# Eight-sequence transformer block on one core: gate denominators, moments, stacks, divisions and projections placed elsewhere in the order of the work, and the first sequence's attention visits put between whole units

## The chip, the cores and the metric

The kernel runs on one core of a Trainium2 chip. Time is device time in microseconds for one execution of the whole program. Three runs of the kernel before took 641.94, 647.98 and 648.69 us; their median, 647.98 us, is the figure to compare with.

## The reference: what is computed

Input is x with 8 sequences of 512 positions and 256 features, float32. Both branches work on the layer norm of x:

```python
xn = _layernorm(x, axis=-1)
s = _L0_attn_ref(xn, in_proj_w, out_proj_w)
g = _silu(_L0_ffn_ref(xn, k0, k1, k2, s0, s1, s2))
return x + s * g

# attention: 16 heads of 16, rotary embedding on q and k
delta = pos[:, None] - pos[None, :]
mask = (delta >= 0) & (delta < 250)
attn = softmax(where(mask, q @ k.T * 16 ** -0.5, min))
s = (attn @ v) @ out_proj_w.T

# feed-forward: weights are +1 or -1, chosen by booleans
h = concatenate([xn, -xn])            # 512
h = relu(s0 * h @ w0) * 2             # 1024
h = relu(s1 * h @ w1) * 2             # 1024
g = s2 * h @ w2                       # 256, then silu
```

The attention is a sliding window: a position sees itself and the 249 before it.

## The kernel before, in words

**Layout.** Everything runs with features on the partitions and the 512 positions along the row. A sequence has 2 chunks of 128 features in and out, and 8 chunks of 128 hidden features.

**Feed-forward.** A hidden layer is computed in units: unit f of `h1` makes hidden chunk f from the normed input, unit f of `h2` makes it from all eight chunks of `h1`. To keep float32 accuracy each operand is split into an f16 high part (`xh`, `h1h`, `h2h`) and a low part of a reduced float32 (`xl`, `h1l`, `h2l`), and each product is done for both. So an `h2` unit is two halves of 8 matmuls of 128x512, high and low (L511). Its result is read by ScalarE (ACT), which writes the high part (L522), and then by VectorE (DVE), which writes the low part (L520) and so releases the bank of the accumulator. The last layer (L562, `z_ps`) makes `gate` u = 0 and 1, one for each output chunk.

**Gate.** silu(g) is g / (1 + exp(-g)). `gate_ready` (L623) does it: load of the residual `xr` (L545, a DMA on the SP queue), exp on ACT into `den` (L627), +1 on GpSimd (POOL, L631), the reciprocal in two halves on DVE (L636), and the product on POOL (L638). There is one `den` buffer, and both gates of a sequence use it.

**Attention.** q and k of a sequence are projected (`ka_ps`, `kb_ps`, `qa_ps`, `qb_ps`, L381), multiplied by the rotary tables on DVE (L397), added up on POOL (L418), split into high and low parts (ACT L434, DVE L441), and written to DRAM (L427). `stack` (L450) loads them back in the arrangement that the scores need, one pair of k and q tiles for each group of heads, four groups. The scores are then done in six visits a sequence (`step`): 12 matmuls into six `sc` banks (L745), six exps on ACT (L770), masks on POOL (L790, L797), and in the next visit the products with v into `po` (L827). `keep` copies `po` out (odd groups on DVE L845 and L846, even ones on ACT L851 and L852). `divisions` then sends the row sums through DRAM to pack them (gather L915, pack L923), inverts them on DVE (L929), unpacks them (L942) and multiplies `V` by them (shuffle on DVE L948, product on POOL L949). `project_o` makes `att_ps` (L959), multiplies it with the gate (DVE L981), adds the residual (POOL L988) and stores (L989).

**Norm of the next sequence.** For all but the first, `load_xT` loads the transposed input, `stats` and `lay_down` compute mean and deviation and write these moments to DRAM (L289), `lay_over` broadcasts them to all partitions as `of_all` (L298, 512 KB), and `norm_turned` does, for each of two chunks c, (x - mean) * rstd on DVE (L309, two operations), `xh` on ACT (L315) and `xl` on DVE (L313).

**The order of the work.** Nothing is scheduled by the compiler. `everything` is a list of pieces (nominal time, cost, function). `run` sorts them by nominal time and calls them in that order; its clock advances by the costs, and what a piece returns is called with a delay after it. The resulting order is kept on each engine: PE, DVE, ACT, POOL and the SP queue each take their instructions strictly as emitted. A sequence has `SEQ` = 42 units of nominal time; an `h1` unit costs `L1` = 0.87, an `h2` unit `L2` = 3.45 (emitted as two halves of 1.725, first the f16 matmuls, then the reduced ones), and a `z` product `L3` = 1.87. In the time of sequence b the engines do the attention and the `h2` units of b, the last layer, the gates and the output of b-1, and norm and projections of b+1. The nominal times of those are in `prepare` (norm, k, q, v), `finish_ffn` and `late` (gates, `att_ps`) and `divisions`.

**Places of the visits.** `attention` puts the six visits evenly among the pieces of its sequence by cost: for b > 0 only in front of a piece whose time is in `quick` (the start of a whole unit), for b = 0 in front of any piece. It puts the four `stack` calls at times derived from the visits; tiles for stacks have two buffers, so a group can be loaded when the last visit of the group two before it has been reached.

**Accumulator banks.** Seven banks of one tag serve `h_ps`, `sc` (six in a visit), `z_ps`, `att_ps` and all projections in turn; an eighth holds `po`. A product on PE can begin when the seventh bank before has been read out, whoever reads it.

Of the kernel before, what the change touches and what calls it, by code (L numbers as in the profile page):

```python
# [34 lines left out]
def tile_attention_times_gated_ffn(  # L35
# [44 lines left out]
    B, T, E = x.shape  # L80
# [140 lines left out]
    SEQ = 42.0  # L221
# [1 line left out]
    states = {}  # L223


    quick = set()

    def warm(count_):

# [223 lines left out]
    def prepare(b, plain=False):  # L453

        if b == 0 or plain:
            at = dict(stats=-40, norm=-38, x=-36, k=0, q=3, v=9.2)
            dp, dv = 1.5, 1.5
        else:

            at = dict(load=9, stats=9, down=10.5, over=12, norm=16.8, k=21.8, q=24.8, v=SEQ + 0.6)  # L460
            if b == 1:
                at.update(load=18.65, stats=15, down=18, over=18.7, norm=24.8, k=26.6, q=28.4)
            dp, dv = 1.5, 0.85
            at = {n: SEQ * (b - 1) + f for n, f in at.items()}
        out = [(at["stats"], 0, lambda: stats(b))]
        if "over" in at:
            out += [
                (at["load"], 0, lambda: load_xT(b)), (at["down"], 0, lambda: lay_down(b)),
                (at["over"], 0, lambda: lay_over(b)),
                (at["norm"], 0, lambda: norm_turned(b, 0)),  # L470
                (at["norm"] + 1.2, 0, lambda: norm_turned(b, 1)),
            ]
        for t in range(NT):
            if "over" not in at:
                out += [
                    (at["norm"] + t, 0, lambda t=t: norm(b, t)),
                    (at["x"] + t, 0.25, lambda t=t: turn_x(b, t, plain)),
                ]
            out.append((at["v"] + dv * t, 0.87, lambda t=t: project_v(b, t)))
        for what in "kq":  # L480
            for n, part in enumerate("ab"):
                if b == 0 and what == "k" and not plain:

                    out += [
                        (-34.3 if n == 0 else -32.95, 0.87, lambda p=part: project(b, "k", p, 0)),
                        (at["k"] + dp * n, 0.87, lambda p=part: project(b, "k", p, 1)),
                    ]
                else:
                    out.append((
                        at[what] + dp * n, 1.75, lambda w=what, p=part: project(b, w, p),  # L490
                    ))
        return out
# [54 lines left out]
    def last(b, u, how):  # L547
        st = states[b]
        f, cols = outputs(b)[u]
        pz = bank(f"z_ps_{b}_{u}")  # L550
        if b + 1 == B:
            pz = pz[:, : T // 2]
        if how == "at once":
            for c in range(NF1):
                nc.tensor.matmul(
                    pz, w2[:, c, ts(f, P)].bitcast(F32), st["h2p"][:, c, cols],
                    start=(c == 0), stop=(c == NF1 - 1),
                )
        else:
            for p in "hl":  # L560
                for c in range(NF1):
                    nc.tensor.matmul(  # L562
                        pz, weights(w2, p, c, ts(f, P)), st["h2" + p][:, c, cols],
                        start=(c == 0 and p == "h"), stop=(c == NF1 - 1 and p == "l"),
                    )
        if cols.start == 0:
            st["gate of", f] = outs.tile([P, T], F32, tag=f"gate{f}", name=f"gate_{b}_{f}")
        gate = st["gate", u] = st["gate of", f][:, cols]
        if how == "final":
            residual(b, u)  # L570
            den = beside(b, u, "den")

            halves = [ts(k, T // 4) for k in range(2)]

            def ends():
                if u == 2:
                    for k in halves:
                        nc.scalar.activation(
                            den[:, k], pz[:, k], AF.Exp, scale=scales[:, 1:2]
                        )  # L580
                    return [(0.1, ready)]
                nc.scalar.activation(den, pz, AF.Exp, scale=scales[:, 1:2])
                nc.scalar.activation(den, den, AF.Identity, bias=1.0)
                return [(0.88, ready)]

            def ready():
                if u == 2:
                    for k in halves:
                        nc.vector.tensor_scalar(den[:, k], den[:, k], 1.0, None, ALU.add)
                        nc.vector.reciprocal(den[:, k], den[:, k])  # L590
                else:
                    nc.vector.reciprocal(den, den)  # L592
                nc.vector.scalar_tensor_tensor(  # L593
                    gate, pz, scales[:, 0:1], den, ALU.mult, ALU.mult
                )

            return [(0.0, ends)]

        def scale():
            nc.vector.tensor_scalar(gate, pz, scales[:, 0:1], None, ALU.mult)  # L600
            if how != "later":
                return [(7.5 if u == 0 else 11.0, lambda: gate_ready(b, u))]

        return [(0.0, scale)]

# [16 lines left out]

    def gate_ready(b, u):  # L623
        st = states[b]
        residual(b, u)
        gate, den = st["gate", u], beside(b, u, "den")
        nc.scalar.activation(den, gate, AF.Exp, scale=-1.0)  # L627
        width = T // 2 if b + 1 == B else T

        def add():  # L630
            nc.gpsimd.tensor_scalar(den, den, 1.0, None, ALU.add)  # L631
            return [(0.9 + 1.1 * k, lambda k=k: invert_(k)) for k in range(2)]

        def invert_(k):
            part = den[:, ts(k, width // 2)]
            nc.vector.reciprocal(part, part)  # L636
            if k == 1:
                return [(1.8, lambda: nc.gpsimd.tensor_tensor(gate, gate, den, ALU.mult))]  # L638

        return [(0.5, add)]  # L640
# [11 lines left out]
    def late(b, u):  # L652

        if b + 1 == B:
            return last_at(b, 3) + L3 + 0.9 * u
        return SEQ * (b + 1) + (33.5 + 6.4 * u if b + 2 < B else 19.2 + 5.0 * u)

    def finish_ffn(b, u, how):
        quick.add(last_at(b, u))
        out = [(last_at(b, u), L3 * (2 if b + 1 < B else 1), lambda: last(b, u, how))]  # L660
        if how == "later":
            out.append((late(b, u) - 4.5, 0, lambda: gate_ready(b, u)))
        return out

    def ffn(b):

        now = SEQ * b + (NT * L3 if b == 0 else 0)
        out = []
        for f in range(NF0):
            quick.add(now)  # L670
            out.append((now, L1, lambda f=f: layer(b, "h1", "x", w0, f)))
            now += L1
            if f % 4 == 3 and b > 0:
                now += 2 * L3
        if b + 1 == B:
            for half in range(2):
                cols = ts(half, T // 2)
                for f in range(NF1):
                    quick.add(now)
                    out.append((  # L680
                        now, L2 / 2,
                        lambda f=f, cols=cols: layer(b, "h2", "h1", w1, f, cols=cols),
                    ))
                    now += L2 / 2
                now += 2 * L3
            return out
        for f in range(NF1):
            quick.add(now)
            for i in range(2):
                out.append(  # L690
                    (now, L2 / 2, lambda f=f, i=i: layer(b, "h2", "h1", w1, f, i, 2))
                )
                now += L2 / 2
        return out
# [172 lines left out]

    def attention(b, among):

        first, end = SEQ * b + (20.6 if b == 0 else 0.0), ends_at(b)  # L870
        inside = sorted((at, cost) for at, cost, _ in among if first <= at < end)
        whole = sum(cost for _, cost in inside)
        times, done = [], 0.0
        places = {}
        for at, cost in inside:
            if at in quick or b == 0:
                places[at] = done
            done += cost
        for n in range(len(steps)):
# [6 lines left out]
        for g in range(NG):  # L886

            at = times[used[g - 2][-1]] + 0.01 if g > 1 else first - (
                3.5 if b == 0 else 4.0 if b == 1 else 9.0
            )  # L890
            if b and g == 1:
                at = first + 0.01
            out.append((at, 0, lambda g=g: stack(b, g)))
# [108 lines left out]
    def divisions(b, pairs=(0, 1)):  # L1002
        out = []
        for pair in pairs:
            if b + 1 < B:
                first = SEQ * b + 30.0 if pair == 0 else SEQ * (b + 1) + 3.0
            else:
                first = SEQ * b + (22.5 if pair == 0 else 33.4)
            pieces = (gather, pack, invert, unpack, divide)
            very_last = b + 1 == B and pair == 1  # L1010
            for f, at in zip(
                pieces, (0.0, 2.0, 4.4, 6.4, 9.0) if very_last else (0.0, 2.4, 5.2, 7.6, 10.6)
            ):
                out.append((first + at, 0, lambda p=pair, f=f: f(b, p)))
        return out
# [183 lines left out]
```

## Time and profile before

| | us |
|---|---|
| median of 3 runs | 647.98 |
| profiled execution | 648.76 |
| span of the profiled execution | 647.0 |
| busy PE (matmul) | 606.3 (94%) |
| busy DVE | 331.4 (51%) |
| busy ACT | 293.1 (45%) |
| busy POOL | 289.8 (45%) |
| mean granted PE clock | 0.976 |

The span is the time from the first to the last instruction in the trace; the rest of the 648.76 us lies around it. The page cuts the span into 40 slices; the digits are the busy share in tenths, and PEclk is the granted clock in tenths:

```profile
PE   7979979999898998989999898999989989899996
DVE  7834324544544554454634556345653655435346
ACT  3745544535345444544436345353444435365511
POOL 2746431456424454245432455344462435625623
PEclk9989989999899998999989999999999999899999
```

PE is nearly full everywhere, with a slice below full about every fifth; the other three are half full, unevenly. After the first sequence the pattern has a period of about 78.5 us, that of one sequence, until the last.

### The profile page before, as it was taken

The numbers are of one execution on the slowest core, as the hardware profiler recorded it, in microseconds if no ns is written. First come the engines' busy times: TensorE is split into PE (matmuls) and PEld (weight loads), VectorE is DVE, ScalarE is ACT, GpSimd is POOL, SyncE is SP. The second block draws the span as 40 slices with busy tenths as digits, with TensorE's granted clock in tenths as the row PEclk, the third lists the DMA queues.
The fourth block names the chain that finished last, engine by engine and source line by source line (L and its number), as shares of the span: only waits on it lengthen the run. The fifth ranks groups of instructions, "written<-read, shape, count | busy, mean of one in ns | idle before, by whom it ended". The sixth has DMA issues, their size and how long they took to land. (4 is left out here: it accounts for less than half of the span.)

```text
span 647.0 us, 10374 instructions
## 1 busy us (share of the span) xinstructions
PE 606.3 (94%) x3788; PEld 374.5 (58%) x3788; DVE 331.4 (51%) x578; ACT 293.1 (45%) x555; POOL 289.8 (45%) x490
## 2 busy tenths in 40 slices
PE   7979979999898998989999898999989989899996
PEld 6644546555565555555555554654546645566785
DVE  7834324544544554454634556345653655435346
ACT  3745544535345444544436345353444435365511
POOL 2746431456424454245432455344462435625623
PEclk9989989999899998999989999999999999899999
DMA  8774443337333463325434263350734408322101
GB/s 267 285 241 147 187 153 113 99 129 249 116 100 99 164 214 117 100 99 226 153 117 125 73 261 117 121 165 31 278 117 147 151 14 305 124 87 83 52 17 59
DMA packets 50086, 92.24 MB, mean 143 GB/s; under 512 B 10992, under 2 KB 18672, under 8 KB 50032
## 3 DMA queue, kind: packets, MB, share of 16 engines
q1 hardware_dynamic: 47600, 89.31, 40.8%
q10 hardware_dynamic: 2432, 2.23, 1.1%
q8 instruction: 31, 0.51, 0.3%
q14 instruction: 23, 0.19, 0.1%
HBM read 53.22 MB, written 38.30 MB: 141 GB/s over the span
## 5 line engine op out<-in xcount | busy, mean ns | idle before, releaser
L770 ACT ACTIVATE p<-sc 128x512 f32<-128x512 f32 (+2 forms) x288 | 149.2, 604 | 62.5 <-PE sc L745 61.9
L790 POOL TENSOR_SCALAR_AFFINE_SELECT p<-p 128x256 f32<-128x256 f32 (+1 forms) x224 | 100.3, 458 | 149.3 <-ACT p L770 144.7
L511 PE MATMUL h_ps<-h1l,w_sb 128*128 128x512 f32 (+1 forms) x576 | 146.7, 396 | 0.0
L511 PE MATMUL h_ps<-h1h,w_sb 128*128 128x512 f16 (+1 forms) x576 | 124.6, 360 | 11.0 <-ACT p L770 9.0
L511 PEld LDWEIGHTS h_ps<-h1l,w_sb 128*128 128x128 f32 x576 | 100.4, 189 | 30.6 <-issue 10.4
L511 PEld LDWEIGHTS <-w_sb 128*128 128x128 f16 x704 | 62.0, 98 | 95.9 <-issue 51.8
L522 ACT ACTIVATE h2h<-h_ps 128x512 f16<-128x512 f32 (+1 forms) x72 | 39.6, 550 | 142.7 <-PE h_ps L511 142.7
L827 PE MATMUL po<-p,v_pad 128*32 128x378 f32 (+4 forms) x1152 | 83.0, 429 | 0.0
L745 PE MATMUL sc<-q,k 64*128 64x378 f32 (+4 forms) x576 | 59.6, 319 | 20.4 <-DVE gate L981 10.3
L636 DVE RECIPROCAL den<-den 128x256 f32<-128x256 f32 (+1 forms) x32 | 52.6, 1645 | 45.8 <-POOL den L631 45.8
L745 PEld LDWEIGHTS sc<-q,k 64*128 64x128 f32 x576 | 45.9, 187 | 44.1 <-issue 23.0
L520 DVE SCALAR_TENSOR_TENSOR h1l<-h_ps,h1h 128x512 fp32r<-128x512 f32 x64 | 43.2, 688 | 48.3 <-ACT h1h L522 48.2
L520 DVE SCALAR_TENSOR_TENSOR h2l<-h_ps,h2h 128x512 fp32r<-128x512 f32 (+1 forms) x72 | 43.9, 611 | 44.5 <-ACT h2h L522 44.5
L522 ACT ACTIVATE h1h<-h_ps 128x512 f16<-128x512 f32 x64 | 37.6, 602 | 53.5 <-PE h_ps L511 53.5
L797 POOL TENSOR_SCALAR_AFFINE_SELECT p<-p 128x256 f32<-128x256 f32 x144 | 59.9, 416 | 0.4 <-POOL p L790 0.4
L511 PE MATMUL h_ps<-xl,w_sb 128*128 128x512 f32 x128 | 52.3, 489 | 0.0
L827 PEld LDWEIGHTS po<-p,v_pad 128*32 128x32 f32 x1152 | 35.4, 124 | 27.8 <-issue 20.4
L638 POOL TENSOR_TENSOR gate<-gate,den 128x512 f32<-128x512 f32 (+1 forms) x16 | 19.3, 1206 | 56.4 <-issue 29.0
L949 POOL TENSOR_TENSOR V<-V,R 128x512 f32<-128x512 f32 x16 | 20.3, 1271 | 48.9 <-DVE R L948 48.9
L511 PE MATMUL h_ps<-xh,w_sb 128*128 128x512 f16 x128 | 38.5, 383 | 0.0
L562 PE MATMUL z_ps<-h2l,w_sb 128*128 128x512 f32 (+1 forms) x144 | 35.7, 389 | 0.0
L418 POOL TENSOR_TENSOR m_ka<-m_ka,m_kb 128x512 f32<-128x512 f32 x16 | 19.9, 1266 | 35.1 <-DVE m_kb L397 35.1
(102 smaller groups left out, 668.8 us busy)
## 6 DMA issues: line engine op xcount, KB each, us to landing
k<-dk SPq DMA_DIRECT2D x64, 256.0 KB
q<-dq SPq DMA_DIRECT2D x64, 256.0 KB
dk<-kh SPq DMA_DIRECT2D x16, 512.0 KB
dk<-m_ka SPq DMA_DIRECT2D x16, 512.0 KB
dq<-qh SPq DMA_DIRECT2D x16, 512.0 KB
dq<-m_qa SPq DMA_DIRECT2D x16, 512.0 KB
x<-in_x_dram SPq DMA_DIRECT2D x30, 128.0 KB
xT<-in_x_t_dram SPq DMA_DIRECT2D x7, 512.0 KB
```

Source lines behind the costliest of these rows:

```text
L418: nc.gpsimd.tensor_tensor(m[:, i], m[:, i], n[:, i], op)
L511: nc.tensor.matmul(ph, weights(w, p, c, ts(f, P)), st[src + p][:, c, cols], start=(k == 0), stop=(k == n - 1),)
L520: nc.vector.scalar_tensor_tensor(lo, ph, 0.0, hi, ALU.max, ALU.subtract)
L522: high = lambda: nc.scalar.activation(hi, ph, AF.Relu)
L562: nc.tensor.matmul(pz, weights(w2, p, c, ts(f, P)), st["h2" + p][:, c, cols], start=(c == 0 and p == "h"), stop=(c == NF1 - 1 and p == "l"),)
L636: nc.vector.reciprocal(part, part)
L745: nc.tensor.matmul(sc[r + (4 if y else 2 * pair)][:, ds(at, n)], st["k", g, pair][row, ts(j, P)], st["q", g, pair][row, ds(j * P + first, n)],
L770: nc.scalar.activation(p, s_, AF.Exp, scale=D ** -0.5)
L790: nc.gpsimd.affine_select(out=block, in_=block, compare_op=ALU.is_ge, fill=0.0, base=0, pattern=[[0, heads], [1, P]], channel_multiplier=-1,)
L797: nc.gpsimd.affine_select(out=block, in_=block, compare_op=ALU.is_ge, fill=0.0, base=-1, pattern=[[0, heads], [-1, beyond]], channel_multi ...
L827: nc.tensor.matmul(po[32 * r : 32 * r + 32, ds(j * P + first, n)], v_columns(j, g, r), place(tiles_, r, y, off, n), start=(j == 0), stop=( ...
L949: return [(0.5, lambda: nc.gpsimd.tensor_tensor(V, V, R, ALU.mult))]
```

## The change

The change alters no operation, tile or buffer. It alters nominal times and so the order of instructions on the engines:

- the residual's load is a piece of its own instead of the start of `gate_ready`;
- `gate_ready` of the middle sequences moves from 4.5 to 6.6 ahead of `late`, of the last but one to 4.6, and `late` of gate 1 from 6.4 to 4.9 units after that of gate 0;
- `norm` of sequences 2 to 7 goes from 16.8 to 18.4, k from 21.8 to 23.0 and q from 24.8 to 26.0; of sequence 1, k from 26.6 to 28.1 and q from 28.4 to 31.6, with the two parts of a projection at nearly one time (dp 0.01);
- the visits of the first sequence begin at 24.7 instead of 20.6 and lie between whole units: the new set `inner` holds the middles of units, which are no longer places for them; its first stacks keep their time (24.7 - 7.6);
- the stacks of group 3 of all but the first sequence come 5 units later;
- the division of pair 0 of the first sequence begins 5 units later, and the last piece (`divide`) of pair 1 moves from 10.6 to 15.0 after its start, but for the last two sequences.

```diff
-    quick = set()
+    quick, inner = set(), set()
...
-            at = dict(load=9, stats=9, down=10.5, over=12, norm=16.8, k=21.8, q=24.8, v=SEQ + 0.6)
+            at = dict(load=9, stats=9, down=10.5, over=12, norm=18.4, k=23.0, q=26.0, v=SEQ + 0.6)
             if b == 1:
-                at.update(load=18.65, stats=15, down=18, over=18.7, norm=24.8, k=26.6, q=28.4)
-            dp, dv = 1.5, 0.85
+                at.update(load=18.65, stats=15, down=18, over=18.7, norm=24.8, k=28.1, q=31.6)
+            dp, dv = (0.01 if b == 1 else 1.5), 0.85
...
             if how != "later":
-                return [(7.5 if u == 0 else 11.0, lambda: gate_ready(b, u))]
+                at = 7.5 if u == 0 else 11.0
+                return [(at, lambda: residual(b, u)), (at, lambda: gate_ready(b, u))]
...
     def gate_ready(b, u):
         st = states[b]
-        residual(b, u)
...
-        return SEQ * (b + 1) + (33.5 + 6.4 * u if b + 2 < B else 19.2 + 5.0 * u)
+        return SEQ * (b + 1) + (33.5 + 4.9 * u if b + 2 < B else 19.2 + 5.0 * u)
...
         if how == "later":
-            out.append((late(b, u) - 4.5, 0, lambda: gate_ready(b, u)))
+            out += [
+                (late(b, u) - (6.6 if b + 2 < B else 4.6), 0, lambda: gate_ready(b, u)),
+                (late(b, u) - 4.2, 0, lambda: residual(b, u)),
+            ]
...
             quick.add(now)
+            inner.add(now + L2 / 2)
...
-        first, end = SEQ * b + (20.6 if b == 0 else 0.0), ends_at(b)
+        first, end = SEQ * b + (24.7 if b == 0 else 0.0), ends_at(b)
...
-            if at in quick or b == 0:
+            if at in quick or b == 0 and at not in inner:
...
-                3.5 if b == 0 else 4.0 if b == 1 else 9.0
+                7.6 if b == 0 else 4.0 if b == 1 else 9.0
             )
+            if b and g == 3:
+                at += 5.0
...
-                first = SEQ * b + 30.0 if pair == 0 else SEQ * (b + 1) + 3.0
+                first = SEQ * b + (30.0 if b else 35.0) if pair == 0 else SEQ * (b + 1) + 3.0
...
-                pieces, (0.0, 2.0, 4.4, 6.4, 9.0) if very_last else (0.0, 2.4, 5.2, 7.6, 10.6)
+                pieces,
+                (0.0, 2.0, 4.4, 6.4, 9.0) if very_last
+                else (0.0, 2.4, 5.2, 7.6, 15.0 if pair and b + 2 < B else 10.6),
```

## The prediction

> **What bounds the kernel now.** I read, in this order, the page's busy shares, the waits of the tensor engine (PE), the timeline of one period, and the windows by clock. PE is busy 606.3 of 647.0 us (94%); no other engine is above 51%. So the time is PE's work plus PE's gaps plus what a lower clock costs. The waits (line, what is waited for: us in total, times, longest) name nearly all gaps:
>
> ```profile
> PE sc L745 <- DVE gate L981: 10.3, 6, 1.7
> PE h_ps L511 <- ACT p L770: 9.0, 6, 1.6
> PE sc L745 <- DMA q<-dq: 7.4, 4, 2.7
> ...
> PE h_ps L511 <- DVE gate L981: 2.0, 6, 0.3
> PE sc L745 <- ACT p L770: 1.5, 1, 1.5
> PE sc L745 <- DVE h2l L520: 0.9, 2, 0.6
> ```
>
> Three of them come six times: they belong to the six middle periods of 78.5 us, where sequence b is computed and b-1 finished. The DMA rows are the first sequence's. One period's timeline (start, us, engine, line, operation; in brackets the gap before it and its releaser):
>
> ```profile
> 285.13 1.89 PE L511 MATMUL h_ps<-h1h,w_sb 128*128 128x512 f16 x8 [1.65 <-ACT p L770]
> ...
> 313.35 1.89 PE L511 MATMUL h_ps<-h1h,w_sb 128*128 128x512 f16 x8 [0.33 <-DVE gate L981]
> ...
> 325.02 0.61 PE L745 MATMUL sc<-q,k 64*128 64x256 f32 x3 [1.72 <-DVE gate L981]
> ...
> 283.39 0.72 ACT L315 ACTIVATE xh<-xT,sgnx 128x512 f16<-128x512 f32 x1 [2.36 <-DVE xT L309]
> ...
> 307.20 1.75 DVE L636 RECIPROCAL den<-den 128x256 f32<-128x256 f32 x1 [3.25 <-POOL den L631]
> ...
> 324.28 0.69 DVE L981 TENSOR_TENSOR gate<-att_ps,gate 128x512 f32<-128x512 f32 x1 [1.44 <-POOL gate L638]
> ```
>
> The reader sees two causes. At 285 PE needs a bank whose exp stands on ACT behind `xh`, which waits for DVE's second pair of `xT`. At 313 and 325 it needs the bank of `att_ps`, whose product waits for the gate chain: exp, +1, two reciprocals, multiplication. After the last of these the windows (busy us of PE, PEld, DVE, ACT, POOL; clock; DMA share; GB/s) show a fourth cost:
>
> ```profile
> 321.84:325.25 3.41, 1.69 (x15) 1.12 (x13) 1.97 (x3) 2.54 (x5) 1.47 (x2) 1.00 0.00 0
> 325.25:328.67 3.42, 3.42 (x39) 1.78 (x41) 0.97 (x3) 0.00 (x0) 3.42 (x6) 0.50 0.39 113
> ```
>
> PE runs at half clock for one window: about 1.7 us lost. This happens nine times: once in each of the six periods, at 325.25 and its like, and at 38.53, 62.43 and 89.73 in the first sequence.
>
> **What the Trainium skill says.** "TensorE: Matmul & The Clock Gate", Part 1, states a half rate (4/8) and a free-running window of 3413 ns: the trace agrees (0.50, 3.41 us). It has the clock fall after an idle window; here a window that still held 1.69 us of PE work was enough, so I use the measurement. Gaps of 1.5 us that a window's edge divides (285.13) did not drop it. The same page gives ScalarE, VectorE and GpSimdE strict first-in, first-out queues: the trace agrees (exp behind `xh`), and this decides every wait below. "SBUF — State Buffer", section "SBUF: two separate sides", has DVE operations with two SBUF inputs and GpSimd operations exclude each other; the trace fits it: two POOL rotations took 3.50 us at 19.24 against 2.52 at 298.90.
>
> **The change part by part: middle periods.** In program order DVE now does all four `xT` (L309) before any `xl`. The second pair ends near 281.8 instead of 283.36, so `xh` and the exps move up 1.55: of 1.50 (9.0/6) about 0.1 stays. The `qb` projection goes behind the second half of unit 3, the first `att_ps` before unit 7 instead of inside it: no PE work is added (four matmuls, 1.88 us, either way). The denominators start earlier: den_0's exp on ACT after unit 3's `h2h`, den_1's between the `h2h` of units 4 and 5. Both chains end before their `att_ps` products, so 0.33 (2.0/6) and 1.72 (10.3/6) go, with the 1.7 of half clock; the `h2l` waits, 0.9/6 = 0.15, go as well. Removed: 1.50 - 0.10 + 0.33 + 1.72 + 1.70 + 0.15 = 5.3 us a period.
>
> **The wait it adds.** den has one buffer, and DVE now holds, in this order: `h2l` of unit 4, den_1's first reciprocal, `h2l` of unit 5, second reciprocal, product 0. Visit 5's last `sc` bank is released by `h2l` 5, so it waits for den_1's +1 on POOL, which is behind the masks of visit 4 and gate_0's multiplication, itself behind den_0. From the end of unit 3 on PE the durations, start to next start in the timeline at 298 to 312, add up: `h2h` 0.5, den exp 0.65, +1 1.49, reciprocal 1.67 (307.20 to 308.87), `m_qb` with rotation 3.28 (from m_qb's first start at 298.14 to 301.42), three masks 1.1, multiplication 1.27, visit 4's other masks 1.9, +1 1.49, reciprocal 1.67, `h2l` 0.66: 15.7. PE's work up to the same bank: `qb` 1.72, visit 4 with values, units 4 and 5 and `att_ps` 11.4, nine of twelve scores 0.75: 13.9. So a stall of about 1.8 to 2.0; with DVE's L441 (1.22 us) in the way of POOL's multiplication, 3.1. I take 2.0. Being unbroken it should mostly drop the clock: 85% of 1.7, 1.45. Queued behind it on PE are only visit 5's three scores and its values, so one stall is paid, not several. A period gains 5.3 - 2.0 - 1.45 = 1.85; six give 11.1.
>
> SP's moves cost nothing there: each of two residual loads goes ahead of a few stores (the first ahead of `m_qa`'s), and an issue takes some 0.4 us on SP, which idles; the order of the group-3 stacks among SP's other issues stays. Without that cover the next stacks would land later, and no middle period shows a wait for one today. `V·R` goes behind visit 2's masks on POOL, well before `att_ps` in the next period.
>
> **First and last sequence.** Visit 0 is now behind unit 2 (3.9 us), so the two DMA waits
>
> ```profile
> 35.41 0.50 PE L745 MATMUL sc<-q,k 64*128 64x378 f32 x4 [1.54 <-DMA q<-dq]
> 37.90 0.81 PE L745 MATMUL sc<-q,k 64*128 64x378 f32 x8 [1.98 <-DMA q<-dq]
> ```
>
> are hidden: 3.52 + 1.7 of half clock = 5.2. The wait of 1.49 at 61.33 with its half clock, 3.2, goes too, since later visits stand between whole units. But ACT's order puts both `xh_1` before the last exp of visit 0. They need the moments broadcast to all partitions, and that transfer, issued at 41.85, is first used at
>
> ```profile
> 45.38 3.12 DVE L309 TENSOR_TENSOR xT<-xT,of_all 128x512 f32<-128x512 f32 x4
> ...
> 41.85 0.34 SPq L298 DMA_DIRECT2D of_all<-d  x1
> ```
>
> so `xT` ends at 48.5, `xh` 0.72 later, the exp at 49.8; visit 1 on PE stands at nine of twelve scores from about 43: 6.9 us of new wait and 1.2 of half clock. (The transfer is 512 KB; "DMA: Bandwidth & Descriptors", section "Anatomy of one DMA", would estimate 2.0 + 1.2 = 3.2 us; the trace's 3.53 to first use agrees.) Group 3's stacks now follow sequence 1's store of `kh` on SP; `kb` is projected ahead of visit 2, they are first used in visit 4, and I cost that at 0. The stacks of sequence 1 still queue on SP behind the stores of `q` and are issued about 82.35 (before: 82.40), so 85.87 and 89.04 with 1.17 + 2.67 become about 2.3 + 1.0, with half clock: 0.6 better. Sum: 5.2 + 3.2 + 0.6 - 8.1 = +0.9, unsure by 4 either way. The last sequence only shifts small pieces (rows earlier, `late` minus 4.6): 0.
>
> **Sum.** Against the profiled execution's 648.76: -11.1 - 0.9 = 636.8. That execution is 0.8 above the median of the runs, 647.98, so I forecast **636.0**.
>
> **Rivals.** *A, no new bound.* The new chain is 1 us shorter than my sum (PE's own times are modelled; 0.4 in `h2h` and masks each would do) and the wait is either absent, 5.3 x 6 + 0.9 = 32.7 (615), or about 1.2 without a drop of clock, 4.1 x 6 + 0.9 = 25.5 (622.5). For it: today's split gaps of 1.5 us keep the clock. Against it: the strict order, and 15.7 against 13.9. *B, slower.* The shared port stretches the chain: rotation 1.0 longer (3.50 against 2.52), multiplication behind L441 1.2, +1 behind a `m_qb` pair 1.3. That is 2.0 + 3.5 = 5.5 of stall, with 1.7 of clock and 0.35 more lost at the next window: 5.3 - 7.5 = -2.2 a period, 661 in the end. It decides from 5.3 + 0.15 - 1.7, some 3.75 us of stall. For it: POOL would be without pause over 10 us; against: these pairs ran beside each other undisturbed at 298 to 301. *C, no net change.* A stall near 3.5, or the first sequence's 6.9 doubled by a late transfer: 645 to 650. That the change doesn't act belongs here: the orders did move, but an `att_ps` wait may only be replaced by its neighbour.
>
> **Chances.** Likeliest 0.56 (628 to 643), A 0.24, C 0.11, B 0.09. The range of 8 in 10, from 613 to 646, holds A, and leaves out B and most of C. Within 1% (6.5 us), about what a measurement of this kernel can tell from no change, is 641.5 to 654.5: C and a little of the likeliest. Faster 0.78, same 0.13, slower 0.09.
>
> **What would show it.** Right: PE's wait for ACT `p` before L511 gone from the periods, no wait for the gate product, six waits of scores for DVE `h2l` of 2 to 3 us with a half-clock window after each, one long wait of scores for ACT `p` between 43 and 50 us, DMA waits only near 85. Wrong: six `h2l` waits under 1 us (A), over 3.7 us (B), or half-clock windows under three in all. If 43 to 50 shows no wait, the first-sequence step is wrong.

## The result, and the profile after

| | before | changed |
|---|---|---|
| median of 20 runs, us | 645.83 | 640.38 |
| lowest and highest, us | 640.11, 649.26 | 638.34, 644.52 |
| profiled execution, span, us | 648.76, 647.0 | 643.67, 641.9 |
| PE busy, us | 606.3 | 600.2 |
| DVE busy, us | 331.4 | 345.8 |
| mean granted clock in the profile | 0.976 | 0.976 |

The ratio is 0.9928, with a 95% interval of 0.9904 to 0.9953: 0.7% faster, where 1.9% was forecast (636.0 against 647.98). The three runs shown with the kernel before lay high; in 20 runs its median is 645.83, 2.2 us lower. The ratios below leave out executions that were more than 1.5% longer than a kernel's fastest; this concerns two of the six of e1, whose ratio is therefore lower than that of the medians.

PE's waits in the kernel after (line, what is waited for: us in total, times, longest):

```profile
PE sc L749 <- DVE h2l L520: 16.0, 6, 2.7
PE sc L749 <- ACT p L774: 7.0, 1, 7.0
PE h_ps L511 <- ACT p L774: 5.8, 6, 1.1
PE sc L749 <- DMA q<-dq: 3.7, 3, 1.8
```

The reader sees a trade. Both rows with the gate product (10.3 and 2.0) are gone. The first row, 2.67 us in each of six periods, is new. The second is the first sequence's, also new. The third was 9.0 and is 5.8. All of PE's gaps of over 0.15 us add up to 32.1 us before and 33.4 after, so the 5.1 us of span come out of PE's busy time, 6.1 us less: less work at half clock (30.6 us before, 27.2 after, worth 1.7), and small waits inside what counts as busy, which the account of the prediction takes up.

The new wait, in the timeline of one period (start, us, engine, line, operation; in brackets the gap before it and what released it), PE first, then DVE, then POOL:

```profile
308.16 0.94 PE L749 MATMUL sc<-q,k 64*128 64x378 f32 x9
311.77 0.79 PE L749 MATMUL sc<-q,k 64*128 64x244 f32 x3 [2.67 <-DVE h2l L520]
...
303.87 2.30 DVE L441 TENSOR_TENSOR m_qa<-m_qa,qh 128x1024 fp32r<-128x1024 f32 x1 [1.47 <-ACT qh L434]
306.09 0.68 DVE L520 SCALAR_TENSOR_TENSOR h2l<-h_ps,h2h 128x512 fp32r<-128x512 f32 x1
309.42 1.75 DVE L636 RECIPROCAL den<-den 128x256 f32<-128x256 f32 x1 [2.65 <-POOL den L631]
311.09 0.63 DVE L520 SCALAR_TENSOR_TENSOR h2l<-h_ps,h2h 128x512 fp32r<-128x512 f32 x1
...
303.81 1.27 POOL L638 TENSOR_TENSOR gate<-gate,den 128x512 f32<-128x512 f32 x1
305.04 1.39 POOL L794 TENSOR_SCALAR_AFFINE_SELECT p<-p 128x256 f32<-128x256 f32 x1
306.39 0.40 POOL L801 TENSOR_SCALAR_AFFINE_SELECT p<-p 128x256 f32<-128x256 f32 x1
...
307.90 1.48 POOL L631 TENSOR_SCALAR den<-den 128x512 f32<-128x512 f32 x1
```

Read it from the end: PE is released by the second `h2l`, which stood behind den_1's reciprocal, which waited 2.65 us for POOL's +1. POOL was late because its mask at 305.04 took 1.39 where its like takes 0.40, and L441 on DVE, beside it, took 2.30: first the multiplication held up L441, then L441 the mask. The times fit one operation waiting for the other to end: the multiplication ends at 305.08, and L441 ends 1.09 us later, which is nearly its whole length where it ran alone (1.23 at 302.72 of the kernel before).

The third row, the wait ahead of unit 2, has its source here (DVE, then POOL):

```profile
277.06 3.73 DVE L309 TENSOR_TENSOR xT<-xT,of_all 128x512 f32<-128x512 f32 x4
...
277.18 1.72 POOL L955 TENSOR_TENSOR V<-V,R 128x512 f32<-128x512 f32 x1 [2.04 <-DVE R L954]
```

`V*R` of the division now runs beside the four `xT`, and both are longer than where they ran alone (2.75 us for four `xT` at 46.30 of the same profile, 1.27 for `V*R`).

The clock, in windows of 3.41 us (busy us of PE, PEld, DVE, ACT, POOL with counts; clock; DMA share; GB/s):

```profile
307.41:310.82 3.41, 1.69 (x11) 0.75 (x9) 1.40 (x1) 1.58 (x3) 1.97 (x3) 1.00 1.00 393
310.82:314.24 3.42, 2.47 (x12) 0.83 (x13) 3.39 (x6) 0.20 (x1) 0.24 (x1) 0.50 0.33 91
314.24:317.65 3.41, 3.41 (x9) 1.58 (x8) 2.28 (x3) 2.40 (x5) 3.41 (x6) 0.50 0.92 293
385.92:389.33 3.41, 2.19 (x13) 1.00 (x11) 0.90 (x1) 1.81 (x4) 2.47 (x4) 1.00 0.98 340
389.33:392.75 3.42, 1.97 (x15) 0.86 (x16) 3.42 (x4) 0.64 (x2) 0.00 (x0) 1.00 0.33 120
```

The same wait of 2.67 us, at 309.10 and at 388.11, costs two windows at half clock in one period and none in another: the edge at 310.82 divides the first into 1.72 and 0.95 us, the edge at 389.33 the second into 1.22 and 1.45. Five of the six periods lose clock.

### The profile page after: what moved, and what is told of

Same layout as the page of the kernel before. It is cut to its first block, busy times and chain, and to the rows that moved or that the text cites. A ratio compares the mean times of both kernels' runs of the same rounds, so it can differ in the third digit from the quotient of the medians.

```text
span 641.9 us, 10381 instructions
## 1 busy us (share of the span) xinstructions
PE 600.2 (93%) x3788; PEld 371.0 (58%) x3788; DVE 345.8 (54%) x578; ACT 293.5 (46%) x555; POOL 290.4 (45%) x490
## 4 chain that ended last, share of the span: by engine, by line
PE 51%; DVE 16%; POOL 11%; DMA 8%; issue 7%; ACT 3%; SPq 3%; ACTq 0%; POOLq 0%; DVEq 0%
PE h_ps L511 24%; PE po L831 7%; PE z_ps L562 6%; DMA of_all<-d 4%; PE sc L749 4%; DVE xT L309 4%; PE v_ps L361 4%; DVE den L636 3%; POOL p L794 3%; POOL den L631 3%; POOL m_ka L418 3%; PE ka_ps L381 2%; PE att_ps L965 2%; PE kb_ps L381 2%; DMA q<-dq 1%
## 5 line engine op out<-in xcount | busy, mean ns | idle before, releaser
L794 POOL TENSOR_SCALAR_AFFINE_SELECT p<-p 128x256 f32<-128x256 f32 (+1 forms) x224 | 103.2, 471 | 141.8 <-ACT p L774 127.3
L511 PE MATMUL h_ps<-h1h,w_sb 128*128 128x512 f16 (+1 forms) x576 | 130.2, 371 | 5.8 <-ACT p L774 5.8
L511 PEld LDWEIGHTS <-w_sb 128*128 128x128 f16 x704 | 63.3, 100 | 97.2 <-issue 55.4
L749 PE MATMUL sc<-q,k 64*128 64x378 f32 (+4 forms) x576 | 56.0, 317 | 26.7 <-DVE h2l L520 16.0
L831 PE MATMUL po<-p,v_pad 128*32 128x378 f32 (+4 forms) x1152 | 74.8, 393 | 0.0
L749 PEld LDWEIGHTS sc<-q,k 64*128 64x128 f32 x576 | 44.2, 189 | 51.0 <-DVE h2l L520 19.2
L801 POOL TENSOR_SCALAR_AFFINE_SELECT p<-p 128x256 f32<-128x256 f32 x144 | 56.4, 392 | 0.3 <-POOL p L794 0.3
L955 POOL TENSOR_TENSOR V<-V,R 128x512 f32<-128x512 f32 x16 | 22.0, 1373 | 55.6 <-DVE R L954 55.6
L831 PEld LDWEIGHTS po<-p,v_pad 128*32 128x32 f32 x1152 | 31.4, 111 | 22.5 <-issue 13.6
L994 POOL TENSOR_TENSOR gate<-gate,xr 128x512 f32<-128x512 f32 (+1 forms) x15 | 18.6, 1238 | 42.4 <-DVE gate L987 42.2
```

Of the source, the lines that this page charges most:

```text
L511: nc.tensor.matmul(ph, weights(w, p, c, ts(f, P)), st[src + p][:, c, cols], start=(k == 0), stop=(k == n - 1),)
L749: nc.tensor.matmul(sc[r + (4 if y else 2 * pair)][:, ds(at, n)], st["k", g, pair][row, ts(j, P)], st["q", g, pair][row, ds(j * P + first, n)],
L794: nc.gpsimd.affine_select(out=block, in_=block, compare_op=ALU.is_ge, fill=0.0, base=0, pattern=[[0, heads], [1, P]], channel_multiplier=-1,)
L801: nc.gpsimd.affine_select(out=block, in_=block, compare_op=ALU.is_ge, fill=0.0, base=-1, pattern=[[0, heads], [-1, beyond]], channel_multi ...
L831: nc.tensor.matmul(po[32 * r : 32 * r + 32, ds(j * P + first, n)], v_columns(j, g, r), place(tiles_, r, y, off, n), start=(j == 0), stop=( ...
```

## The experiments

Ratios are to the kernel before on the same chip, with 95% intervals; "runs" counts those of the kernel itself.

| kernel | ratio | interval | median us, runs |
|---|---|---|---|
| changed | 0.9928 | 0.9904 to 0.9953 | 640.38, 20 |
| e1 divide back | 0.9883 | 0.9840 to 0.9927 | 642.12, 6 |
| e2 den_1 later | 0.9529 | 0.9502 to 0.9555 | 616.09, 6 |
| e3 norm 1 later | 0.9799 | 0.9776 to 0.9823 | 634.64, 5 |
| e4 all three | 0.9400 | 0.9378 to 0.9421 | 608.09, 5 |
| e5 gates alone | 0.9816 | 0.9778 to 0.9855 | 635.47, 4 |
| e6 first sequence alone | 0.9996 | 0.9975 to 1.0016 | 646.48, 20 |
| e7 norm alone | 1.0000 | 0.9982 to 1.0019 | 646.57, 20 |
| e8 no low part of q | 0.9738 | 0.9681 to 0.9794 | 628.27, 4 |
| e9 moments earlier | 0.9374 | 0.9344 to 0.9404 | 605.49, 5 |
| e10 gates, den_1 later | 0.9608 | 0.9562 to 0.9654 | 621.38, 4 |

### Is the new wait only the place of h2l behind the reciprocal? (e2)

```diff
-                (late(b, u) - (6.6 if b + 2 < B else 4.6), 0, lambda: gate_ready(b, u)),
+                (late(b, u) - (6.6 - 1.8 * u if b + 2 < B else 4.6), 0, lambda: gate_ready(b, u)),
```

> The changed kernel with gate 1's denominator 1.8 units later (late minus 4.8 instead of 6.6), which puts unit 5's h2l on DVE ahead of den_1's first reciprocal. Theory (the 2.67 us wait of visit 5's last scores, with the half clock after it, is only the place of h2l behind the reciprocal): the wait is gone, each of six periods is 2.7 + 1.6 = 4.3 us shorter, 25 us in all, ratio to the kernel before about 0.955. Rival (the gate chain of POOL and DVE is simply too long and the wait moves): gate 1's product is late by 1 to 2 us ahead of the next sequence's scores, with its half clock, as in the kernel before; ratio 0.98 to 0.99.

Measured: 0.9529. PE's waits begin

```profile
PE sc L749 <- ACT p L774: 5.9, 1, 5.9
PE h_ps L511 <- ACT p L774: 5.2, 6, 1.1
PE sc L749 <- DMA q<-dq: 3.2, 2, 2.4
```

No row for `h2l`, none for the gate product: den_1's chain, begun one `h2` unit later, is still in time. A period takes 73.1 us on average against 77.7 in the changed kernel (from the first `xh` matmul of sequence 1 to that of sequence 7, divided by six). None of their waits drops the clock any more. The two engines still hold each other up there (L441 takes 2.31 us, the mask beside it 1.42), but no bank waits behind them. So the place of den_1's chain decides whether there is a wait, and the rival falls; how long the wait is, where there is one, is the next question.

### What made it 2.67 and not 2.0? (e8)

This kernel leaves out the subtraction that makes the low part of q in sequences 2 to 7; zeros are stored in its place.

```diff
+        if what == "q" and b > 1:
+            for turn in range(2):
+                for j in range(2):
+                    place = 2 * (2 * turn + (1 ^ turn)) + j
+                    nc.sync.dma_start(st["dram", what][:, place, :], raw_xT["zero"])
+            return
         lo = m.bitcast(F32R)
         nc.vector.tensor_tensor(lo, m, st["hi"].bitcast(F32), ALU.subtract)
```

> The changed kernel, leaving out for sequences 2 to 7 the subtraction on DVE that makes the low part of q (zeros are stored in its place), so that DVE has no two-input operation beside POOL's gate multiplication and masks. Theory (this subtraction, 2.30 us instead of 1.22, and the mask after it, 1.39 instead of 0.41, block each other and so lengthen the new chain by 1.0): the mask takes 0.4 us, the wait for h2l falls from 2.67 to about 1.7 in each of six periods, 6 us in all or more where the clock then holds, ratio to the kernel before about 0.983. Rival (the chain is long for other reasons): the wait stays at 2.5 or more, ratio 0.991 to 0.994.

Measured: the wait fell to 10.1/6 = 1.68 us, and the mask behind the multiplication (second line) takes 0.41:

```profile
PE sc L755 <- DVE h2l L526: 10.1, 6, 1.7
```

```profile
298.74 1.29 POOL L644 TENSOR_TENSOR gate<-gate,den 128x512 f32<-128x512 f32 x1
299.98 0.41 POOL L800 TENSOR_SCALAR_AFFINE_SELECT p<-p 128x256 f32<-128x256 f32 x1
```

So the 1.0 us is the collision of L441 with the multiplication and the mask, as expected. The ratio, 0.9738, is better than the wait alone explains: in the profile all six waits of 1.7 us are divided by a window's edge and the clock holds. The other DMA pieces that store the zeros are not separated from this.

### What keeps the wait ahead of unit 2? (e1)

```diff
-                else (0.0, 2.4, 5.2, 7.6, 15.0 if pair and b + 2 < B else 10.6),
+                else (0.0, 2.4, 5.2, 7.6, 10.6),
```

> The changed kernel with one time put back: the last piece of pair 1's division at 10.6 instead of 15.0, so that R's shuffle on DVE and V*R on POOL come ahead of visit 2's masks again and no longer beside the four xT operations. Theory (POOL's V*R and DVE's two-input xT hold each other up): the four xT take about 3.1 us instead of 3.7, PE's wait for ACT p ahead of unit 2 falls from 0.97 to at most 0.4 us in each of six periods, 3.5 us in all, ratio to the kernel before about 0.988. Rival (the wait is left because xT starts late, on the landing of of_all): xT still starts at the landing, the wait stays near 1.0 us and the ratio at 0.993.

Measured: the wait fell from 0.97 to 1.7/6 = 0.28.

```profile
PE sc L749 <- DVE h2l L520: 16.0, 6, 2.7
...
PE h_ps L511 <- ACT p L774: 1.7, 6, 0.3
```

The four `xT` and `V*R` in this run:

```profile
278.42 3.25 DVE L309 TENSOR_TENSOR xT<-xT,of_all 128x512 f32<-128x512 f32 x4 [0.55 <-DMA k<-dk]
...
276.37 1.27 POOL L955 TENSOR_TENSOR V<-V,R 128x512 f32<-128x512 f32 x1 [5.15 <-DVE R L954]
```

`V*R` is over before `xT` begins, and `xT` takes 3.25 us instead of 3.73. On the mean of the six periods the four `xT` take 3.18 instead of 3.71 us, and they start 1.54 us ahead of visit 2's scores instead of 1.39. So of the 0.69 us gained about 0.53 is the collision, and 0.15 the earlier start. It isn't free of collisions: `xT` now runs beside visit 2's masks, of which the last two take 0.85 and 1.08 there instead of 0.41 and 0.63. A gain in time is not shown: the interval overlaps the changed kernel's, and the median of all six executions, 642.12, is 0.993 of the kernel before on that chip (646.74). In this profiled execution (648.50 us) each wait for `h2l` cost two windows at half clock, and only its waits are used.

### Is the 7 us of the first sequence ACT's order? (e3)

```diff
-                at.update(load=18.65, stats=15, down=18, over=18.7, norm=24.8, k=28.1, q=31.6)
+                at.update(load=18.65, stats=15, down=18, over=18.7, norm=26.8, k=28.1, q=31.6)
```

> The changed kernel with the norm of sequence 1 at 26.8 instead of 24.8, so that ACT does the last exp of visit 0 and the h2h of unit 3 ahead of both xh. Theory (the 6.96 us wait at 50 us is ACT's order alone): it goes, the projection ka waits for xT instead, about 2.5 us, net 4 to 6 us with the half clock, ratio about 0.985. Rival (the first sequence waits for the moments' transfer in any case, so the wait only changes its name): less than 2 us, ratio 0.991 to 0.994.

Measured: 0.9799, better than expected. PE waits 3.0 us ahead of `ka` instead of 6.96 ahead of the scores (the view names no releaser; the second `xT` ends at 47.93 and `ka` begins at 48.03), and the first `xh` matmul of sequence 1 comes at 88.98 instead of 93.45 us: 4.5 us, as expected. The rest is in the middle periods, in which every engine has the changed kernel's order to the last instruction. They take 77.7 and 76.25 us in turn in this profile. The windows show why (busy times and clock as above), first around the wait for `h2l` in a short period, at 227.05, then in a long one, at 303.06:

```profile
225.20:228.61 3.41, 1.85 (x12) 0.90 (x10) 1.25 (x1) 1.57 (x3) 2.13 (x3) 1.00 0.99 381
228.61:232.02 3.41, 2.31 (x17) 0.97 (x18) 3.41 (x5) 0.97 (x2) 0.08 (x1) 1.00 0.36 95
303.71:307.12 3.41, 1.40 (x12) 0.57 (x13) 3.41 (x3) 0.58 (x3) 0.00 (x0) 1.00 0.40 153
307.12:310.53 3.41, 3.41 (x9) 1.59 (x8) 3.31 (x6) 2.53 (x5) 2.58 (x3) 0.50 0.94 294
```

In one, the wait is divided 1.56 to 1.10 by an edge and the clock stays whole; in the other 2.01 us lie in one window and the next runs at half. How many periods pay depends on where they fall on the grid of windows. That a shift of the first sequence improves this in general is not shown.

### Which part of the change does what? (e5, e6, e7)

Each is the kernel before with one part of the diff shown above: e5 the gates (`gate_ready`, `residual`, `late`), e6 the first sequence (`inner`, 24.7, 7.6, k and q of sequence 1, dp 0.01, division at 35.0), e7 the middle sequences' norm, k, q, the stacks' 5.0 and the division's 15.0.

> The kernel before with only the gates' part of the change: residual apart, gate_ready at late minus 6.6 (4.6), late of gate 1 at 4.9 after gate 0. Theory (this part both removes the gate waits and brings the h2l wait): PE's waits for the gate product (2.05 us a period) are gone, a wait of scores for h2l of 2 to 3 us with a half clock after it takes their place, the wait of 1.5 ahead of unit 2 stays; ratio to the kernel before 0.995 to 1.005. Rival (the h2l wait needs the moved projections too): no h2l wait, 3.5 to 4 us less a period, ratio about 0.965.

> The kernel before with only the first sequence's part: visits from 24.7 between whole units, k and q of sequence 1 later, the first division later. Theory (what the first visits gain, the 7 us wait behind xh takes back): the first sequence is within 1 us of before, ratio 0.998 to 1.003. Rival (the 7 us come only with the other parts): the two DMA waits and their half clock are saved, 4 to 5 us, ratio 0.993.

> The kernel before with only the middle sequences' norm, k and q later, group 3's stacks 5 units later and pair 1's last division piece at 15.0. Theory: the wait of 1.5 us ahead of unit 2 falls to about 1.0, both gate waits and their half clock stay; 3 us in all, ratio about 0.995. Rival (the later projections push the gate chain, which is still in its old place, later): the gate waits grow by 1 us or more and the ratio is over 1.005.

Measured: 0.9816, 0.9996 and 1.0000. In e5 neither ratio came: the wait for `h2l` comes with the gates, as the theory has it, but it is shorter.

```profile
PE h_ps L511 <- ACT p L773: 9.0, 6, 1.6
PE sc L748 <- DVE h2l L520: 8.9, 6, 1.5
```

It is 1.48 us here, and four of the six hold the clock. With `qb` still ahead of unit 3's second half, `m_qb` and its rotation are done before den_0's +1; in the whole change `m_qb` stands between den_0's two reciprocals and the rotation between its +1 and its multiplication, and the wait is 2.67. L441 collides with the multiplication here too, the other way round: L441 starts first and takes 1.16 us, the multiplication 2.08. e6 is as the theory: the visits' two DMA waits are gone, a wait of 6.0 us for ACT stands in their place. In e7 the wait ahead of unit 2 fell as the theory has it, to between 0.7 and 1.1 us, and the gate waits stayed; but neither ratio came, since each period has a new wait of 1.0 us for `h2l`:

```profile
PE sc L745 <- DVE gate L983: 10.4, 6, 1.8
...
PE sc L745 <- DVE h2l L520: 6.0, 6, 1.0
PE h_ps L511 <- ACT p L770: 4.8, 6, 1.1
```

The product of the three ratios is 0.981; the whole change has 0.9928. So the parts do not add, and about 1% is lost between them. The change of the `h2l` wait from 1.48 to 2.67 us is about that much (6 x 1.2 = 7.1 us); that the later projections make it so is read from the orders above and was not tried by itself.

### What are the parts worth once the wait is gone? (e4, e10, e9)

e4 has the edits of e1, e2 and e3 together; e10 is e5 with the edit of e2; e9 is e4 with

```diff
-            at = dict(load=9, stats=9, down=10.5, over=12, norm=18.4, k=23.0, q=26.0, v=SEQ + 0.6)
+            at = dict(load=9, stats=8, down=9.5, over=11, norm=18.4, k=23.0, q=26.0, v=SEQ + 0.6)
```

> The three edits together (division of pair 1 back at 10.6, gate 1's denominator 1.8 units later, norm of sequence 1 at 26.8). Theory: the gains add, since they lie in different places: 3.5 + 25 + 5 us below the changed kernel, ratio to the kernel before about 0.94. Rival: once these waits are gone something else (the clock's windows, stacks, a product) binds and less than two thirds of the sum arrives, ratio over 0.96.

> The kernel before with the gates' part alone, and gate 1's denominator 1.8 units later (late minus 4.8). Theory (gate waits and h2l wait both go, and neither the moved norm and projections nor the first sequence's part is needed for it): per period only the 1.5 us ahead of unit 2 is left, about 4 us less than before, ratio about 0.96. Rival (with the projections in their old place the new order binds elsewhere): a wait for h2l or the gate product of over 1 us in each period, ratio 0.975 or above.

> The version with all three edits, with the moments of sequences 2 to 7 one unit earlier (stats 8, down 9.5, over 11). Theory (in that version the 0.85 us ahead of unit 2 is left because PE is ahead of the moments' transfer: DVE idled 0.8 us for of_all): xT starts as early as its DVE place allows, the wait falls to 0.3 us or less, 3 to 4 us in all, ratio to the kernel before about 0.935. Rival (the eight statistics operations now stand ahead of h1l on DVE and PE waits for that instead): ratio 0.940 or above.

Measured: 0.9400, 0.9608, 0.9374, near the theory each time. e10 shows that the gates with one time set otherwise bring 3.9% with no other part. In e4 the wait ahead of unit 2 was back at about 0.85 in five of six periods: PE was now early enough for DVE to idle 0.8 us for the moments' broadcast. Moving that by one unit removed the wait. e9 has the lowest time here, but its interval overlaps e4's, so that a gain over e4 is not shown. Two of its periods (columns as above, all five engines):

```profile
87.16:159.21 72.05, 72.05 (x453) 43.12 (x449) 42.00 (x68) 35.00 (x66) 32.74 (x53) 1.00 0.38 134
159.21:231.25 72.04, 72.04 (x452) 43.11 (x448) 41.95 (x68) 35.00 (x66) 34.94 (x59) 1.00 0.46 156
```

PE is busy 72.05 of 72.05 us at full clock: what remains in these periods is PE's own work. For comparison, one period of the changed kernel, then one of the kernel before:

```profile
93.45:171.12 77.67, 74.16 (x452) 43.79 (x448) 43.12 (x70) 35.23 (x66) 34.20 (x54) 0.98 0.39 138
...
93.54:171.97 78.43, 74.88 (x453) 44.39 (x449) 40.51 (x68) 35.11 (x66) 34.41 (x58) 0.98 0.39 131
```

## Why the prediction was right in kind and wrong in size

The prediction is taken by its own steps, on the profiled executions (span 647.0 to 641.9, -5.1; forecast -12.0):

- **The wait it adds** was right in place, cause and count: six waits of scores for `h2l` behind den_1's reciprocal. The term "I take 2.0" measured 2.67: 4.0 us in six periods. The prediction had L441 in POOL's way as its upper bound, 3.1, and chose the end without it. e8 shows that this collision is 1.0 us. As a reason for that choice it says that "these pairs ran beside each other undisturbed at 298 to 301". In the trace only the rotation and `m_qb` did (the rotation took 2.52); L441 ran at 297.01 and 302.72 and the multiplication at 311.29, so the pair that mattered had never stood together.
- **"About 0.1 stays"** of the wait ahead of unit 2 measured 0.97: 5.2 us. The failed step is the one that let `V*R` go behind visit 2's masks at no cost. I checked when its result is needed, and not what runs beside it on DVE, whose operations and POOL's hold each other up; e1 shows 0.7 of the 0.87, of which 0.5 is in the length of `xT` and the rest in its start.
- **The removed terms** 0.33, 1.72 and 0.15 went as said.
- **The half clock**, 85% of the periods, measured five of six. That the next window may stay at half too (310.82 to 317.65) was not in the sum: PE's work at half clock in the six periods went from 20.4 to 19.5 us, where 17.4 was forecast. At half speed that is 1.1 us.
- **The first sequence**: +0.9 was forecast, and sequence 1 starts on PE at 93.45 instead of 93.54, +0.1. The new wait was set at 6.9 and is 6.96, in part by luck. The prediction took the broadcast's first use, 3.5 us after its issue, for its landing; but there `xT` began as DVE came free of an `h2l` (44.69 to 45.38). In the kernel after, where DVE idled for it, `xT` began 4.8 us after the issue (41.54 to 46.30), and PE's wait began 0.4 later than assumed. The half clock after the wait was set at 1.2 and cost 2.2 (4.5 us of PE's work at half clock). The DMA waits at 85 were set at 2.3 + 1.0 and are 1.61 + 1.77.
- **Not in the sum**: small waits between scores that count as busy. From the first of twelve scores to the next other matmul, with the waits of the list above taken off and time at half clock halved, a visit takes 1.00 us where nothing holds it up. Before, visits 0 and 3 took 1.33 on average in the middle periods; after, 1.01 and 1.00. That is 1.9 + 2.0 us in six periods; visit 0's share goes with the gate wait, which stood in that visit. Visit 5, with the new wait, gained nothing (1.32 and 1.36), so it is 3.7 us in all. One visit 3, before and after:

```profile
123.10 1.50 PE L745 MATMUL sc<-q,k 64*128 64x378 f32 x12
...
123.03 1.07 PE L749 MATMUL sc<-q,k 64*128 64x378 f32 x12
```

-12.0 + 4.0 + 5.2 + 0.8 + 1.1 - 3.7 = -4.6, against -5.1; the other 0.5 is open. The direction was right, and the likeliest case was the one that came; two terms, both mis-sized mainly because DVE and POOL hold each other up, took 9.2 us of the 12.0. That the error is not larger is luck, since the 3.7 us were not foreseen. By the prediction's own yardstick, 1%, the 0.7% would not have been told from no change; it took 20 runs of each kernel. Rival B named the shared port as what could stretch the new chain, but with 3.5 us from it; 1.0 came.

## What to carry to other kernels

When an operation is moved on DVE or POOL, ask what will run beside it on the other of the two, and not only who waits for its result: a placement that was costed at nothing and a collision that was left out of the sum took 0.7 and 1.0 us here, every period. Ask then whether anything waits behind it: in e2 the second collision is still there, and no wait. When a chain is started earlier to meet its consumer, look for the short operation that now stands behind the chain's slow step in a strict queue; starting the chain a little later was worth 4% here. And where PE is 93% busy, a wait has two prices, its length and the clock after it, so the second should be counted from window edges and not from the length alone, with a margin: near half a window of idle time both outcomes occur in these traces.

## What the runs showed of the hardware that was not expected

- The clock drops after windows in which PE was still half busy; no whole idle window is needed. In the traces here 1.69 us busy of 3.41 dropped it, 1.85 with 2.31 in the next did not, nor 2.19 with 1.97. No one busy share decides it: a window with 1.93 us busy dropped the clock at 384.57 of e5 and not at 538.17, and one with 1.76 did not drop it at 535.82 of e3. Nor does one share decide the return. At 310.82 a window with 2.47 us busy at half clock was followed by a second one at half, and so was one with 3.14 at 469.38 of e1; after 3.09 at 47.71 of e3 the clock came back. The Trainium skill ("TensorE: Matmul & The Clock Gate", Part 1) speaks of an idle window; the measurement decides.
- The windows lie on one grid through an execution: the kernel before's windows at half clock begin between 38.53 and 560.77 us, 153 windows apart. In its six periods they are 78.51 us apart, 23 windows, so each period met the grid at the same place and paid each time. In e3 the wait meets the grid at different places, and periods of the same order took 77.7 and 76.25 us.
- The kernel before spread over 640 to 649 us in 20 runs. A part of that goes with the clock: in the 59 executions of it that ran beside e1 to e10 the mean granted clock lay between 0.974 and 0.984, and the six with 0.981 or more had a median of 643.6 us, the others one of 646.7. How much of the spread is the grid was not tried.
- The exclusion of DVE and POOL works in both directions and on masks too: L441 of q took 2.10 us on the mean of eight in the changed kernel, 1.30 before (16.8 and 10.4 us in all), and a mask beside it 1.39 instead of 0.40; in e5, where L441 came first, it was the multiplication that took 2.08 instead of 1.27. This agrees with the Trainium skill ("SBUF — State Buffer", section "SBUF: two separate sides").
